# Weight loads and table clears in shorter DRAM rows, in a graph-attention and relational graph-convolution kernel

## The chip, the cores and the metric

The kernel runs on one core of a Trainium2 chip. The time is device microseconds (us) of one execution, taken as the median of several executions. All arithmetic is float32. In the profile PE is TensorE, DVE is VectorE, ACT is ScalarE, POOL is GpSimd and SP is SyncE, which in this kernel only issues DMAs. One queue of the DMA engines, q1, carries what SP issues; another, q0, carries what POOL issues. Sixteen DMA engines serve all queues. MB and GB are decimal, KB is 1024 bytes.

## The reference

Two layers run one after the other on 384 nodes with 12,672 edges, and each adds its result to its input. The first is attention in 16 heads with a mask built from the edges; the second is two relational graph convolutions with six relations that share four basis matrices.

```python
h = jnp.maximum(_layernorm(x), 0.0)                       # x: 384 x 1024
q = h @ wq.T + bq;  k = h @ wk.T + bk;  v = h @ wv.T + bv
q2, k2, v2 = heads(q @ wiq.T + biq), heads(k @ wik.T + bik), heads(v @ wiv.T + biv)
mask = full((N, N), -inf).at[src, dst].set(softplus(edge_type_weights)[edge_type - 1])
attn = softmax(q2 k2^T / 8 + mask)                        # per head
x = x + (attn v2) @ wo.T + bo

h = jnp.maximum(_layernorm(x), 0.0)
y = relu(h @ w_in + b_in)                                 # 384 x 768
for l in range(2):
    W = einsum('rb,bio->rio', comp[l], basis[l])          # 6 relations, 4 bases
    msg = einsum('ni,rio->rno', y, W)[edge_type, src] / counts[edge_type, dst]
    y = batchnorm(relu(segment_sum(msg, dst) + y @ root[l] + bias) + y)
x = x + layernorm(y @ w_out + b_out)
```

## The kernel before

**Sparse edges become dense tables in DRAM.** `mtab0` to `mtab3` hold the attention mask (384 x 384 cells each); `atab0` and `atab1` hold, for each relation, how many edges go from one node to another (6 x 384 x 384 cells each). SP first clears them from SBUF tiles (`clear_mask`, L182, and `clear`, L274: 576 KB for each DMA). Then POOL scatters 128 edges at a time: 99 DMAs of `put_mask` (L264) and 99 of `put_count` (L269). The second kind adds to the cell, four bytes for each edge. A `put_count` on one of the two tables waits until the earlier one on the same table has landed.

**POOL's queue is in program order.** It issues the mask scatters and 14 count scatters while the projections run, then loads the mask (L311), then issues the other 85 count scatters, and only then loads the adjacency counts into SBUF as the tile `A` (six relations, 576 KB each): `atab1` is copied into `A[:, r]` (L834 for r = 0, 1, L838 for the others) and `atab0` is added to it by an accumulating DMA (L836). Between these, `add_up(r)` (L339, L340) sums the three node blocks of `A[:, r]` on POOL into the tile `sum`.

**TensorE needs these sums.** In the first graph convolution (layer 0 in what follows), `share(r)` (L345) is a pair of matmuls that adds `sums[r]` over the partitions; the result gives the reciprocal edge count, with which DVE scales `A[:, r]`. The dictionary `between` places `share(0)`, `share(1)`, `share(2)` inside the products of basis 2 of layer 0, `share(3)` after them, `share(4)` and `share(5)` inside the products of basis 3. PE runs in program order too, so a share that isn't ready holds up all that follows. After basis 3, `mix` (L330, L332) combines the six relations into the four matrices `At`.

**Weights come through one queue and one pool.** `wload` (L76 to L81; its DMA is L80) takes one of five buffers of `wpool` and issues a load on SP. A projection of the attention layer uses four loads of 1 MB, a basis matrix or `root` three loads of 768 KB (a third of 768 x 768), `w_out` three of 1 MB. `w_in` is loaded by two DMAs of 1.5 MB at L734. SP waits at a load until its buffer is free, and the loads run ahead of the products that use them. The products are recursive (Strassen-like) ones: DVE first forms differences of the weights (L380, L555, L771, L911, L913, L919), then PE multiplies. The basis products are L969 and L963.

**Layout.** On the host each weight is arranged so that one load gives each of the 128 partitions one contiguous row: 8 KB for the attention projections and `w_out`, 12 KB for `w_in`, 6 KB for `basis` and `root`. A clear writes 4.6 KB (1,152 floats) for each partition.

Of the kernel before, what the change touches and what calls it, by code (L numbers as in the profile page):

```python
# [10 lines left out]
F32 = mybir.dt.float32  # L11
# [18 lines left out]
HN = N // 2  # L30
R = 6
# [11 lines left out]
MCELLS, ACELLS = N * N, N * R * N  # L43
# [8 lines left out]
def gnn_kernel(ctx: ExitStack, tc: tile.TileContext, out, x, edges, chunks, cols, rows, small,  # L52
               wq, wk, wv, wiq, wik, wiv, wo, w_in, basis, root, w_out):
    nc = tc.nc
# [5 lines left out]
    wpool = ctx.enter_context(tc.tile_pool(name="wpool", bufs=5))  # L60
# [9 lines left out]
    def next_bank(name, among=range(8)):  # L70

        i = next(i for i in ring if i in among)
        ring.remove(i)
        ring.append(i)
        return bank(i, name)

    def wload(src, name):

        w = wpool.tile([P, *src.shape[1:]], F32, tag="w", name=name)
        nc.sync.dma_start(w, src)  # L80
        return w  # L81

    turn = [0]
# [88 lines left out]
    mtab = [tables.tile([MCELLS + P, 1], F32, name=f"mtab{i}") for i in range(MT)]  # L172
    atab = [tables.tile([ACELLS + P, 1], F32, name=f"atab{i}") for i in range(2)]
    keys_d = tables.tile([PAD, P], I32, name="keys_d")

    def edge_steps(ep, none, zero):
# [2 lines left out]
        nc.sync.dma_start(small_sb, small.to_broadcast([P, 52]))  # L179

        def clear_mask(i):
            nc.sync.dma_start(mtab[i][:MCELLS, :].rearrange("(p f) o -> p (f o)", p=P), none)  # L182

        clear_mask(0)
        clear_mask(1)
# [11 lines left out]
        part = ep.tile([P, 1], F32, name="part")  # L197
# [73 lines left out]
                                         count[:, 1, c:c + 1], None, compute_op=ALU.add)  # L271

        def clear(i, r):
            nc.sync.dma_start(atab[i][:ACELLS, :].rearrange("(r p f) o -> r p (f o)", p=P, r=R)[r], zero)  # L274

        counts = enumerate(j * PER + r for r in range(PER) for j in range(tables_in(r)))

# [78 lines left out]
    with ExitStack() as inner:  # L356
        ap = inner.enter_context(tc.tile_pool(name="attn", bufs=2))

        def act_tile(name):
            return ap.tile([P, KD, N], F32, tag="T", name=name, bufs=4)  # L360
# [32 lines left out]
        def project(w, src, bias, name, on_part=None, on_start=None):  # L393

            dst = act_tile(name)
            for part in range(4):
                wt_ = wload(w[part], f"w_{name}")
                ps = [next_bank(f"ps_{name}") for _ in range(2)]

                cuts = (slice(0, HN), slice(HN, N)) if src is hT and part == 0 else (slice(0, N),)  # L400
                for c in cuts:
                    for o in range(2):
                        for k in range(KD):
                            nc.tensor.matmul(ps[o][:, c], wt_[:, k, o * P:(o + 1) * P], src[:, k, c],  # L404
                                             start=(k == 0 and c.start == 0), stop=(k == KD - 1 and c.stop == N),
                                             skip_group_check=True)
                        if on_start:
                            on_start = on_start()
                for o in range(2):
                    oc = part * 2 + o  # L410
                    nc.scalar.activation(dst[:, oc, :], ps[o][:, :N], AF.Identity,
                                         bias=cols_sb[:, bias + oc:bias + oc + 1])
                fill(1)
                if on_part:
                    on_part(part, dst)
            return dst

        def fill(n):

            for _ in range(n):  # L420
                if next(steps, "end") == "end":
                    break

        boB = ap.tile([P, D], F32, name="boB", bufs=1)
        with tc.tile_pool(name="edge", bufs=1, side="right") as ep:
            none = ep.tile([P, NT * N], F32, tag="V1", name="none")
            nc.gpsimd.memset(none, 8.0 * NEG)
            zero = ep.tile([P, NT * N], F32, tag="V2", name="zero")
            nc.gpsimd.memset(zero, 0.0)
            xn = ap.tile([P, NT, D], F32, tag="T", name="xn", bufs=4)  # L430
            with tc.manual_schedule(engines={mybir.EngineType.Activation}):
# [6 lines left out]
                half = lambda t: lambda j: x_sb[:, t, j * 512:(j + 1) * 512]  # L438
# [27 lines left out]
            def prepare():  # L466

                name, w, _, part = plan[len(loaded)]
                wt_ = wload(w[part], f"w_{name}")
                loaded.append([[wt_[:, i * 4:i * 4 + 4, o * P:(o + 1) * P] for i in range(2)] for o in range(2)])  # L470
                S.append(output_sums(loaded[-1], ep.tile([P, 4, 4, P], F32, tag="S", name="S", bufs=2)))

# [10 lines left out]
            for n, (name, w, bias, part) in enumerate(plan):  # L483
                src = {"q2": q, "k2": made.get("k")}.get(name, hT)
                if part == 0:
                    dst = made[name] = act_tile(name)
# [5 lines left out]
                a, s = loaded[n], S[n]  # L492
# [34 lines left out]

            wv2 = [[wload(wiv[half, j], "w_v2") for j in range(2)] for half in range(2)]  # L530

            def va(i, j):

# [87 lines left out]

        prA = keep.tile([P, KD, N], F32, tag="hT", name="prA")
        prB = soft.tile([P, KD, N], F32, name="prB")
        w_o = [[wload(wo[half, j], "w_o") for j in range(2)] for half in range(2)]
        attT = act_tile("attT")
        scale = 1.0 / math.sqrt(HD)
        STEPS = (H // 2) * NT
# [87 lines left out]
        for g in range(STEPS + 1):  # L715
            f = g + LEAD
            if g < STEPS:
                turn_probs(g)
            if f < STEPS:
                exponents(f)  # L720
            if f - 1 in total:
                normalise(f - 1)
            if f + 1 < STEPS:
                scores(f + 1)
            if g == STEPS:
                ps_y = next_bank("ps_y", (0,))
                multiply_o(ps_y, 2, 0, range(KD - 1))
            if g > 0:
                gather(g - 1)
            if f + 2 == STEPS:  # L730

                w_x = [act_tile("w_x") for _ in range(2)]
                for half in range(2):
                    nc.sync.dma_start(w_x[half], w_in[half])  # L734
                w_first = [wload(basis[0, 0, part], "w_c") for part in range(3)]
                w_first += [wload(basis[0, 1, part], "w_c") for part in range(2)]
        soft_stack.close()
        xtp = ctx.enter_context(tc.tile_pool(name="xtp", bufs=2, side="right"))

# [6 lines left out]
        a = [[[w_x[oc // 3][:, i * 4:i * 4 + 4, oc % 3 * P:(oc % 3 + 1) * P] for i in range(2)]  # L746
              for oc in (2 * p, 2 * p + 1)] for p in range(3)]
# [108 lines left out]
        for p in range(3):  # L856
            s = S[p % 2]
# [32 lines left out]
    with tc.tile_pool(name="conv", bufs=1) as cp:  # L890
# [31 lines left out]
        w_first = [w_first[:3], w_first[3:]]  # L922

        def load_basis(l, b):
            w = w_first.pop(0) if w_first else []
            return w + [wload(basis[l, b, part], "w_c") for part in range(len(w), 3)]


        def shares(*rs):
# [17 lines left out]
        w = load_basis(0, 0)  # L947
        T = weight_sums(w)
        for l in range(L):
# [3 lines left out]
            for b in range(B):  # L953
# [38 lines left out]
                if b + 1 < B:  # L992
                    w = load_basis(l, b + 1)
# [1 line left out]
                go_between(l, b, 4)  # L995


            w = [wload(root[l, part], "w_c") for part in range(3)]
            XN = xtp.tile([P, KC, N], F32, tag="XT", name="XN")
            pr = [next_bank("ps_c", [i for i in range(8) if i not in kept])[:, :N] for _ in range(KC)]  # L1000
            for k in range(KC):
# [8 lines left out]
            if l + 1 < L:  # L1010
# [4 lines left out]
                w = load_basis(l + 1, 0)  # L1015
# [136 lines left out]

        for t in range(NT):
            nc.gpsimd.tensor_tensor(x_sb[:, t, :], x_sb[:, t, :], rowsB[:, 2, :], ALU.add)  # L1154
        w = [wload(w_out[part], "w_out") for part in range(3)]
        hf_ = cp.tile([P, NT, D], F32, tag="H", name="hf")
        for t in range(NT):
            hf = hf_[:, t, :]
# [26 lines left out]
def _by_outputs(w, n):  # L1185

    *lead, i, o = w.shape
    w = w.reshape(*lead, i // P, P, n, o // n)
    m = len(lead)
    return w.transpose(*range(m), m + 2, m + 1, m, m + 3)  # L1190


def _by_rows(w, n):

    *lead, i, o = w.shape
    w = w.reshape(*lead, n, i // P // n, P, o)
    m = len(lead)
    return w.transpose(*range(m), m, m + 2, m + 1, m + 3)


def _by_inputs(w):

    i, o = w.shape
    return w.reshape(2, i // P // 2, P, 2, o // 2).transpose(3, 0, 2, 1, 4)


def _column(v):

    return v.reshape(-1, P).T
# [35 lines left out]
```

## Time and profile before

| | |
|---|---|
| median of 3 runs | 732.62 us (730.12 to 734.74) |
| the profiled execution, its own time | 729.42 us |
| its span in the trace | 727.6 us |
| DVE busy | 515.2 us (71%) |
| POOL busy | 311.9 us (43%) |
| ACT busy | 157.6 us (22%) |
| granted TensorE clock, mean | 0.99 |
| bytes moved by DMA | 91.00 MB, mean 125 GB/s |
| queue q1 (issued by SP) | 17,678 packets, 78.44 MB, 30.5% of 16 engines |
| queue q0 (issued by POOL) | 21,296 packets, 9.60 MB, 11.2% of 16 engines |

PE is the busy engine, so a change in the time has to come from a moment at which PE isn't working, or is working slower. The table says only how much of the span each engine used; where PE stands still, and for whom, is read from the views of waits, of the chain that ended last and of the time line. A packet in the DMA views is one piece of a transfer on one DMA engine. For SP's loads the counts show that it is one contiguous row: three basis loads of 128 rows of 6 KB each appear as 384 packets of that size, and 48 small ones, 16 for each load.

### The profile page before, as it was taken

Reading aid. Unit: us, or ns where it says so; the run is one execution under the profiler, and the core shown is the slowest. Engines: PE = TensorE matmul, PEld = TensorE weight load, DVE = VectorE, ACT = ScalarE, POOL = GpSimd, SP = SyncE. Lnnn points to the kernel's source line nnn. Section 1 sums busy time; section 2 is a strip of 40 time slices with the busy share of each in tenths; the row PEclk is TensorE's granted clock in tenths of the full one; section 3 lists DMA queues with packets and bytes.
Section 4 is the critical chain, followed back from the end, with each engine's and each line's share of the span. In section 5 each row is a group of like instructions: output and inputs, shape, how many; then the busy total and the mean of one; then the engine's idle time right before and its main releaser. Section 6 shows DMA issues by size and latency. Waiting matters only on the chain.

```text
span 727.6 us, 8832 instructions
## 1 busy us (share of the span) xinstructions
PE 703.3 (97%) x3228; PEld 528.8 (73%) x3228; DVE 515.2 (71%) x1307; ACT 157.6 (22%) x360; POOL 311.9 (43%) x239
## 2 busy tenths in 40 slices
PE   8999999999999999999999959999999999999995
PEld 7759999999996444488975535558975555579943
DVE  5886697969876799777444338899878676506756
ACT  3211111111112587300211115201131111011100
POOL 1366677778676688586785654100000000030000
PEclk9999999999999999999999989999999999999998
DMA  8786786274535522634324699221103213700001
GB/s 298 263 337 203 232 253 212 55 239 135 172 81 154 144 3 1 217 44 96 37 1 130 178 221 250 91 83 44 43 1 130 79 57 125 292 11 1 1 29 58
DMA packets 40024, 91.00 MB, mean 125 GB/s; under 512 B 19644, under 2 KB 26912, under 8 KB 35758
## 3 DMA queue, kind: packets, MB, share of 16 engines
q1 hardware_dynamic: 17678, 78.44, 30.5%
q0 software_dynamic: 21296, 9.60, 11.2%
q10 hardware_dynamic: 1008, 2.41, 0.9%
q8 instruction: 25, 0.41, 0.2%
q14 instruction: 17, 0.14, 0.1%
HBM read 79.27 MB, written 11.16 MB: 124 GB/s over the span
## 4 chain that ended last, share of the span: by engine, by line
PE 84%; DVE 9%; DMA 3%; ACT 2%; POOL 1%; issue 1%; SPq 0%; DVEq 0%; ACTq 0%
PE ps_g L969 11%; PE ps_k L386 10%; PE ps_c L1061 9%; PE ps_g L963 9%; PE ps_v L386 8%; PE ps_q L404 6%; PE ps_q L386 5%; PE ps_f L1167 4%; DVE At L332 4%; PE ps_y L386 3%; PE ps_c L1003 3%; PE ps_x L386 3%; DMA A<-atab 2%; PE ps_o L691 2%; PE ps_s L646 2%; PE ps_pT L680 2%
## 5 line engine op out<-in xcount | busy, mean ns | idle before, releaser
L269 POOL DMA_INDIRECT atab<-count,at x99 | 166.2, 1679 | 59.1 <-DMA atab<-count,at 32.2
L264 POOL DMA_INDIRECT mtab<-m_val,at x99 | 104.9, 1060 | 62.3 <-issue 25.2
L1154 POOL TENSOR_TENSOR x_sb<-x_sb,room 128x1024 f32<-128x1024 f32 x3 | 7.0, 2352 | 177.6 <-DMA room<-in_rows 177.6
L332 DVE SCALAR_TENSOR_TENSOR At<-A,small_sb,At 128x1152 f32<-128x1152 f32 x40 | 53.6, 1411 | 0.0
L969 PE MATMUL ps_g<-w_c,XT 128*128 128x384 f32 x144 | 49.2, 496 | 0.0
L963 PE MATMUL ps_g<-T,S 128*128 128x384 f32 x144 | 49.1, 486 | 0.0
L969 PE MATMUL ps_g<-w_c,XN 128*128 128x384 f32 x144 | 47.7, 487 | 1.1 <-DVE XN L1091 1.1
L404 PE MATMUL ps_q<-hT,w_q 128*128 128x384 f32 (+1 forms) x160 | 43.4, 436 | 1.4 <-DVE hT L97 1.4
L969 PEld LDWEIGHTS ps_g<-w_c,XT 128*128 128x128 f32 x144 | 28.1, 195 | 19.8 <-issue 1.8
L969 PEld LDWEIGHTS ps_g<-w_c,XN 128*128 128x128 f32 x144 | 27.3, 190 | 20.2 <-DVE XN L1091 1.4
L963 PEld LDWEIGHTS ps_g<-T,S 128*128 128x128 f32 x144 | 27.3, 190 | 19.2 <-ACT H L975 0.4
L404 PEld LDWEIGHTS ps_q<-hT,w_q 128*128 128x128 f32 x160 | 30.2, 200 | 14.1 <-ACT hT L90 1.7
L1061 PE MATMUL ps_c<-At,H 128*128 128x192 f32 x216 | 36.4, 326 | 0.0
L1061 PEld LDWEIGHTS ps_c<-At,H 128*128 128x128 f32 x216 | 35.4, 190 | 0.5
L386 PE MATMUL ps_k<-T,S 128*128 128x192 f32 x192 | 35.1, 326 | 0.0
L1091 DVE TENSOR_TENSOR XN<-XN,ps_c 128x192 f32<-128x192 f32 x38 | 12.5, 349 | 30.8 <-ACT XN L1047 19.7
L386 PEld LDWEIGHTS ps_k<-T,S 128*128 128x128 f32 x192 | 31.9, 190 | 0.0
L1167 PE MATMUL ps_f<-w_out,XN 128*128 128x512 f32 (+1 forms) x84 | 31.1, 531 | 0.0
L253 DVE SCALAR_TENSOR_TENSOR same<-keys,key,weigh 128x128 f32<-128x128 int32 x99 | 28.0, 348 | 0.9 <-DVE same L253 0.9
L659 DVE CUSTOM_DVE_ANT_0 s<-ps_s,mask 128x384 f32<-128x384 f32 x48 | 24.5, 549 | 5.2 <-PE ps_s L646 5.2
L253 DVE SCALAR_TENSOR_TENSOR same<-cells,own,later 128x128 f32<-128x128 int32 x99 | 27.9, 350 | 0.4
L1167 PEld LDWEIGHTS ps_f<-w_out,XN 128*128 128x128 f32 x84 | 15.9, 190 | 14.9 <-issue 14.3
(298 smaller groups left out, 1418.3 us busy)
## 6 DMA issues: line engine op xcount, KB each, us to landing
w_c<-in_basis SPq DMA_DIRECT2D x24, 768.0 KB
atab<-zero SPq DMA_DIRECT2D x12, 576.0 KB
A<-atab POOLq DMA_DIRECT2D x12, 576.0 KB
w_c<-in_root SPq DMA_DIRECT2D x6, 768.0 KB
w_q<-in_wq SPq DMA_DIRECT2D x4, 1024.0 KB
w_q<-in_wiq SPq DMA_DIRECT2D x4, 1024.0 KB
w_k<-in_wk SPq DMA_DIRECT2D x4, 1024.0 KB
w_k<-in_wik SPq DMA_DIRECT2D x4, 1024.0 KB
```

Of the source, the lines that this page charges most:

```text
L253: nc.vector.scalar_tensor_tensor(same, row[:, n, :], mine[:, c:c + 1], times, ALU.is_equal, ALU.mult, accum_out=count[:, i, c:c + 1])
L264: nc.gpsimd.indirect_dma_start(mtab[c // PER][:, :], bass.IndirectOffsetOnAxis(at[:, 0, c:c + 1], 0), m_val[:, c:c + 1], None)
L269: nc.gpsimd.indirect_dma_start(atab[0 if i < 11 else i % 2][:, :], bass.IndirectOffsetOnAxis(at[:, 1, c:c + 1], 0), count[:, 1, c:c + 1], ...
L332: nc.vector.scalar_tensor_tensor(At[:, b], A[:, r], w, At[:, b], ALU.mult, ALU.add)
L386: nc.tensor.matmul(ps, a[:, k, :], b[:, k, :], start=start and k == 0, stop=(k == 3), skip_group_check=not start)
L404: nc.tensor.matmul(ps[o][:, c], wt_[:, k, o * P:(o + 1) * P], src[:, k, c], start=(k == 0 and c.start == 0), stop=(k == KD - 1 and c.stop ...
L659: nc.vector.tensor_tensor_reduce(s[j], ps[:, :N], mask8[:, t, :], -scale, 3.0e38, ALU.add, ALU.min, tops[:, j:j + 1])
L963: nc.tensor.matmul(ps, x[:, c], y(c), start=start and c == 0, stop=(c == 2), skip_group_check=not start)
L969: nc.tensor.matmul(ps, block(XT, n, i)[:, c], w[c][:, i, o * HC:(o + 1) * HC], start=(first and c == 0), stop=(c == 2 and (i == 1 or ps is ...
L1003: nc.tensor.matmul(pr[o], w[k // 2][:, k % 2, o * P:(o + 1) * P], XT[:, k, :], start=(k == 0), stop=(k == KC - 1))
L1061: nc.tensor.matmul(ps, x[:, c], y[:, c], start=start and c == 0, stop=stop and c == 5, skip_group_check=True)
L1167: nc.tensor.matmul(p, XT[:, k, t * P:(t + 1) * P], w[k // 2][:, k % 2, c0:c1], start=(k == 0), stop=(k == KC - 1))
```

## The change

`wload` now gets the shape of the tile beside the source, and `load_rows` reads a source of shape (n, 128, size) as n short rows for each partition, in the order of the partition's row. On the host `_short` stores such a source: `wk`, `wv`, `wiq`, `wik`, `wiv` and `wo` in rows of 512 floats (2 KB), `w_in` and `basis` in rows of 384 floats (1.5 KB). `wq`, `root` and `w_out` keep their layout and are loaded as before. The clears of the tables write three rows of 384 floats for each partition in place of one of 1,152. Bytes, destinations in SBUF, the number of DMAs and the order of all instructions on every engine stay the same.

```diff
-    def wload(src, name):
-
-        w = wpool.tile([P, *src.shape[1:]], F32, tag="w", name=name)
-        nc.sync.dma_start(w, src)
+    def load_rows(dst, src):
+
+        if len(src.shape) == 3 and src.shape[1] == P:
+            n, _, size = src.shape
+            nc.sync.dma_start(dst.rearrange("p k o -> p (k o)").rearrange("p (n s) -> p n s", n=n),
+                              src.rearrange("n p s -> p n s"))
+        else:
+            nc.sync.dma_start(dst, src)
+
+    def wload(src, shape, name):
+        w = wpool.tile([P, *shape], F32, tag="w", name=name)
+        load_rows(w, src)
         return w
...
         def clear_mask(i):
-            nc.sync.dma_start(mtab[i][:MCELLS, :].rearrange("(p f) o -> p (f o)", p=P), none)
+            nc.sync.dma_start(mtab[i][:MCELLS, :].rearrange("(c p f) o -> p c (f o)", p=P, c=NT),
+                              none.rearrange("p (c f) -> p c f", c=NT))
...
         def clear(i, r):
-            nc.sync.dma_start(atab[i][:ACELLS, :].rearrange("(r p f) o -> r p (f o)", p=P, r=R)[r], zero)
+            nc.sync.dma_start(atab[i][:ACELLS, :].rearrange("(r c p f) o -> r p c (f o)", p=P, c=NT, r=R)[r],
+                              zero.rearrange("p (c f) -> p c f", c=NT))
...
                 for half in range(2):
-                    nc.sync.dma_start(w_x[half], w_in[half])
-                w_first = [wload(basis[0, 0, part], "w_c") for part in range(3)]
-                w_first += [wload(basis[0, 1, part], "w_c") for part in range(2)]
+                    load_rows(w_x[half], w_in[half])
+                w_first = [wload(basis[0, 0, part], (2, DC), "w_c") for part in range(3)]
+                w_first += [wload(basis[0, 1, part], (2, DC), "w_c") for part in range(2)]
...
+def _short(w, size):
+
+    *lead, _, a, b = w.shape
+    w = w.reshape(*lead, P, a * b // size, size)
+    m = len(lead)
+    return w.transpose(*range(m), m + 1, m, m + 2)
...
-        **{k: _by_outputs(g0(k).T, 4) for k in ("wq", "wk", "wv", "wiq", "wik")},
-        **{k: _by_inputs(g0(k).T) for k in ("wiv", "wo")},
-        "w_in": _by_outputs(g1("w_in"), 2),
-        **{k: _by_rows(g1(k), 3) for k in ("basis", "root", "w_out")},
+        "wq": _by_outputs(g0("wq").T, 4),
+        **{k: _short(_by_outputs(g0(k).T, 4), 512) for k in ("wk", "wv", "wiq", "wik")},
+        **{k: _short(_by_inputs(g0(k).T), 512) for k in ("wiv", "wo")},
+        "w_in": _short(_by_outputs(g1("w_in"), 2), HC),
+        "basis": _short(_by_rows(g1("basis"), 3), HC),
+        **{k: _by_rows(g1(k), 3) for k in ("root", "w_out")},
```

The other calls of `wload` get the shape of their tile in the same way.

More of the change, by code (lines that the diff above doesn't have):

```diff
@@ L396, in project @@
             for part in range(4):
-                wt_ = wload(w[part], f"w_{name}")
+                wt_ = wload(w[part], (KD, 2 * P), f"w_{name}")
                 ps = [next_bank(f"ps_{name}") for _ in range(2)]
@@ L468, in prepare @@
                 name, w, _, part = plan[len(loaded)]
-                wt_ = wload(w[part], f"w_{name}")
+                wt_ = wload(w[part], (KD, 2 * P), f"w_{name}")
                 loaded.append([[wt_[:, i * 4:i * 4 + 4, o * P:(o + 1) * P] for i in range(2)] for o in range(2)])
@@ L526, in gnn_kernel @@
             q2, k2, v = made["q2"], made["k2"], made["v"]
-            wv2 = [[wload(wiv[half, j], "w_v2") for j in range(2)] for half in range(2)]
+            wv2 = [[wload(wiv[half, j], (4, 512), "w_v2") for j in range(2)] for half in range(2)]
             def va(i, j):
@@ L623, in gnn_kernel @@
         prB = soft.tile([P, KD, N], F32, name="prB")
-        w_o = [[wload(wo[half, j], "w_o") for j in range(2)] for half in range(2)]
+        w_o = [[wload(wo[half, j], (4, 512), "w_o") for j in range(2)] for half in range(2)]
         attT = act_tile("attT")
@@ L925, in load_basis @@
             w = w_first.pop(0) if w_first else []
-            return w + [wload(basis[l, b, part], "w_c") for part in range(len(w), 3)]
+            return w + [wload(basis[l, b, part], (2, DC), "w_c") for part in range(len(w), 3)]
         def shares(*rs):
@@ L995, in gnn_kernel @@
                 go_between(l, b, 4)
-            w = [wload(root[l, part], "w_c") for part in range(3)]
+            w = [wload(root[l, part], (2, DC), "w_c") for part in range(3)]
             XN = xtp.tile([P, KC, N], F32, tag="XT", name="XN")
@@ L1154, in gnn_kernel @@
             nc.gpsimd.tensor_tensor(x_sb[:, t, :], x_sb[:, t, :], rowsB[:, 2, :], ALU.add)
-        w = [wload(w_out[part], "w_out") for part in range(3)]
+        w = [wload(w_out[part], (2, D), "w_out") for part in range(3)]
         hf_ = cp.tile([P, NT, D], F32, tag="H", name="hf")
```

## The prediction

> **What bounds the kernel now.** I read four views, from the whole to one moment. First the busy times and what PE waits for (engine, line, releaser: us in total, times, longest).
>
> ```profile
> PE 703.3 (97%) x3228; PEld 528.8 (73%) x3228; DVE 515.2 (71%) x1307; ACT 157.6 (22%) x360; POOL 311.9 (43%) x239
> ```
>
> ```profile
> PE ps_cnt L345 <- POOL sum L340: 7.3, 2, 6.3
> PE ps_q L404 <- DVE hT L97: 1.4, 1, 1.4
> ...
> PE ps_v L386 <- ACT v L502: 1.3, 1, 1.3
> ```
>
> PE stands still for only 24.3 us, some 11 of them before its first products and after its last, and in no row does it wait for a weight. The one large wait is for POOL's sums of A: `share(0)` and `share(1)`. Next PE's time line there (start, us, what, idle before):
>
> ```profile
> 416.96 2.10 PE L963 MATMUL ps_g<-T,XT 128*128 128x384 f32 x6
> 425.32 1.65 PE L345 MATMUL ps_cnt<-sum,ones 128*128 128x384 f32 x2 [6.26 <-POOL sum L340]
> 426.76 5.34 PE L969 MATMUL ps_g<-w_c,XT 128*128 128x384 f32 x12
> 433.17 0.91 PE L345 MATMUL ps_cnt<-sum,ones 128*128 128x384 f32 x2 [1.07 <-POOL sum L340]
> 433.92 4.03 PE L969 MATMUL ps_g<-w_c,XT 128*128 128x384 f32 x12
> ```
>
> Without the stall, the group that starts at 433.92 would start after six products (1.94 from start to start), two shares (0.65 each, as at 437.79) and twelve products (3.87): 416.96 + 1.94 + 0.65 + 3.87 + 0.65 = 424.07. The stall costs 433.92 - 424.07 = **9.85 us**. Besides the waits this holds the slow clock that follows them: twelve products take 5.34 in place of 4.03, and the windows view grants 0.75 and 0.56 at 420 to 430.
>
> The chain that ended last shows what made the sums late (start, us, what):
>
> ```profile
> 407.47 0.81 POOL A L834
> 408.28 5.52 DMA A<-atab
> 413.80 1.43 issue
> 415.23 0.78 POOL A L836
> 416.01 11.62 DMA A<-atab
> ```
>
> POOL reaches the loads of A only at 407.47, since its 99 count scatters come first, and then the loads land slowly. POOL's own time line shows why it is so late:
>
> ```profile
> 389.07 1.55 POOL L269 DMA_INDIRECT atab<-count,at  x1 [0.30 <-issue]
> 391.30 1.56 POOL L269 DMA_INDIRECT atab<-count,at  x1 [0.68 <-DMA atab<-count,at]
> 398.07 1.72 POOL L269 DMA_INDIRECT atab<-count,at  x1 [5.22 <-DMA atab<-count,at]
> ```
>
> An undisturbed scatter follows the last after 0.30 us. Here one waits 5.22 for an earlier one, while SP's three basis loads of 388.77 to 390.06 land.
>
> **What the Trainium skill says.** "DMA: Bandwidth & Descriptors", section "Queues, rings and completion order": each DMA engine goes round robin over the queues that have work, a whole packet at a time. The trace agrees and shows what a packet is. In 295 to 296, beside `w_in` (12 KB rows), and in 299 to 300, beside the start of a basis load (6 KB), the DMA view has
>
> ```profile
> q1 hardware_dynamic: 40, 0.39, 96.5%
> q0 software_dynamic: 40, 0.00, 6.8%
> ...
> q1 hardware_dynamic: 48, 0.38, 95.0%
> q0 software_dynamic: 48, 0.00, 8.1%
> ```
>
> So each 4-byte packet of a scatter waits for one whole row of a weight. SP loads whose rows are short already exist: the key broadcasts of L241, in 1.5 KB runs, give in 112 to 113
>
> ```profile
> q1 hardware_dynamic: 232, 0.37, 100.1%
> q0 software_dynamic: 98, 0.00, 12.4%
> ```
>
> that is, five times as many turns in a us at nearly the same bytes.
>
> Same page, "Why small descriptors are slow (HBM only)": about 3 cycles for each packet beside one for each 32 bytes, and 32 bytes of metadata. From that I estimate 51/48 against 195/192 cycles, 4.6% more for 1.5 KB rows than for 6 KB, and 1.6% more for metadata. The trace is rougher: basis loads run at some 400 GB/s, the key broadcasts between 228 and 377, though these read the same few DRAM rows for every partition.
>
> "TensorE: Matmul & The Clock Gate", section on the HAM clock gate: an idle window of about 3.4 us halves the clock until a busy one has passed. The 6.26 us gap and the 0.56 after it agree.
>
> **The change part by part.**
>
> *Scatters beside weight loads.* From 230 to 407 POOL waits longer than 0.30 for a scatter twelve times beside a load of the changed weights: 0.81, 1.44, 1.36, 1.74 (`wo`), 5.71, 1.57 (`w_in` and basis), 0.64, 0.95, 1.37, 2.25, 0.68, 5.22 (basis). The sum is 23.74, less 12 x 0.30 = 20.1 us. Rows get 4 times shorter (`w_in` 8 times). If each wait shrinks with them, a quarter stays, 5 us, and POOL arrives 15 us earlier. The other bound: of the wait around 391 some 2.4 us pass from the end of the issue (390.6) to the scatter's first packet (393.0); if that entry doesn't shrink, some seven bursts keep 1.4 each over the usual 1, and 10 us are won. I take 12: the loads of A start near 395.
>
> *Loads of A.* In 413.7 to 418 the accumulating load issued at 412.41 gets 27 packets, the basis loads issued from 410.06 get 276; it lands at 423.2, after 10.8. The one issued at 433.06, with no basis load in flight, is used at 439.9, after 6.8. With POOL 12 us ahead the first accumulation is issued near 400, ahead of the 410 loads; the last (442.55, landed 455.0 beside `root`, whose 6 KB rows stay) comes near 430, ahead of `root`'s loads. I count nothing more for either; both are margin.
>
> *Deadlines.* Sums 0 to 5 were ready at 425.3, 433.1, 437.2, 442.0, 448.7, 458.1. A PE without stalls asks for them at 418.9, 423.4, 427.9, 436.3, 443.0, 447.6. They must come earlier by 6.4, 9.7, 9.3, 5.7, 5.7 and 10.5. Twelve us meet all, so the stall goes whole: **-9.85 us**. Next late is DVE's mix (L332, 26.6 us in the chain from 471) beside `root`'s products; it starts when basis 3 ends, moves with PE, and keeps PE's small waits of 0.34 and 0.78.
>
> *Weights landing later.* Three basis loads issued at 555.89 move 2.36 MB by 563; the first is needed by DVE (L911) at 562.52, the same in the other stages: 6.6 us for 786 KB. At 400 GB/s that is 2.0 us of transfer, at the slowest key rate (228) 3.4, with about 1.5 before and after it: no stall. The projections' loads have 9 us or more (`wv` part 3: issued 174.24, used 185.08). Beside A's loads, which take half the turns, the 410.06 load gets perhaps 150 GB/s, 5.2 us, and may come 1 us after DVE's 416.69; PE needs its rows at 424.1. Zero.
>
> *Issue on SP.* A load of 512 pieces takes 0.38 us to issue (keys at 36.69), one of 128 takes 0.33; SP has idle time everywhere. *Clears*: 4.6 KB rows become 1.5 KB on SP's queue, beside mask scatters that end by 211, while DVE first reads the mask at 225. *Start*: `wq` stays. All zero.
>
> Sum: the profiled execution took 729.42, span and 1.8 around it; less 9.85 that is 719.6. The median of the runs shown stands 3.2 higher, 732.62, which would give 722.8. Part of those 3.2 may be a longer stall of the same kind, which would go too. I forecast **722 us**.
>
> **Rivals.**
> 1. *Half the way.* The waits shrink less, or earlier loads of A fall on the burst of 389 to 396 and delay it in turn; A moves 4 to 8 us. For: sum 5 needs 10.5, the largest shift of all. Against: two margins left uncounted. 725 to 730.
> 2. *Nothing moves.* A queue's turn might in truth be bounded by what the engine has fetched ahead, in bytes, so that short rows gain no turns. For: the 2.4 us of entry and the 27 packets, which plain alternation doesn't explain. Against: 232 and 98 beside the keys. About 732.
> 3. *Slower.* The short rows of one partition are taken as one packet after all, so a scatter's piece waits behind a whole load's share, while short rows also move slower: at 300 in place of 400 GB/s every burst lasts a third longer. Scatter waits follow the bursts, 20.1 x 1/3 = 6.7 later, and all of it reaches PE, because the sums already decide there. 739. It loses against the before from the point at which short rows cost more rate than they win turns. Against: the counts beside the keys again.
> That the rows don't get shorter in the transfer is excluded as far as the keys' 1.5 KB packets show the same form of load.
>
> **How the numbers follow.** Forecast 0.72, half 0.11, nothing 0.09, slower 0.08. About 1%, 7.3 us, is what a measurement can tell from no change. The forecast's own spread, 718 to 726, lies mostly beyond that: 0.68 of faster, with a few of rival 1's cases; the rest of both and the nothing case are the same, 0.24; slower 0.08. The range reaches from 717.5 (the stall gone in the lower runs, some 2 us of other small waits too) to 731 (all of the half cases, some of the nothing ones).
>
> **What would show it.** PE's wait at L345 for POOL disappears and the clock stays at 1.00 in 415 to 435; the first L834 is issued near 395; waits of L269 for its own DMA fall from 32.2 us to some 10; q1 has over 100 packets in a us beside basis loads, q0 the same where scatters run. If L834 stays near 407, the turns were not won; if it comes early and PE still waits at L345, the loads of A are at fault; if PE or DVE waits for a weight, the rate is.

## The result, and the profile after

| | before | changed kernel |
|---|---|---|
| median of 20 runs each | 730.0 us (724.98 to 736.25) | 726.79 us (720.17 to 730.59) |
| ratio, 95% interval | | 0.9963 [0.9941, 0.9986] |
| measured again later (e11), 23 and 12 runs | 728.47 us | 725.44 us, 0.9949 [0.9924, 0.9974] |
| span of the profiled execution | 727.6 us | 725.1 us |

A ratio need not be the quotient of the medians beside it: the medians are of all executions, and the ratio leaves out those more than 1.5% above the fastest of their kernel, three of e3's eleven and of e4's eight, four of e6's twenty and of e7's twelve, one of e5's fourteen.

The change wins some 3 us where 10 were forecast. The lines of the changed kernel stand some ten further down: L269 is now L278, L345 is L355, L834 is L844. First the busy times on the page and then what PE waits for (engine, line, releaser: us in total, times, longest):

```profile
PE 701.5 (97%) x3228; PEld 527.8 (73%) x3228; DVE 515.1 (71%) x1307; ACT 157.6 (22%) x360; POOL 308.3 (43%) x239
```

```profile
PE ps_cnt L355 <- POOL sum L350: 8.0, 2, 6.7
PE ps_q L414 <- ACT hT L98: 1.4, 1, 1.4
```

The one large wait of before is still there, two times, and no shorter (7.3 before). PE's time line at the place of the stall (start, us, what, idle before):

```profile
413.82 2.10 PE L973 MATMUL ps_g<-T,XT 128*128 128x384 f32 x6
422.62 1.65 PE L355 MATMUL ps_cnt<-sum,ones 128*128 128x384 f32 x2 [6.71 <-POOL sum L350]
424.07 5.45 PE L979 MATMUL ps_g<-w_c,XT 128*128 128x384 f32 x12
430.81 0.91 PE L355 MATMUL ps_cnt<-sum,ones 128*128 128x384 f32 x2 [1.29 <-POOL sum L350]
431.56 4.03 PE L979 MATMUL ps_g<-w_c,XT 128*128 128x384 f32 x12
```

By the sum used for before, the stall is now 431.56 - (413.82 + 1.94 + 0.65 + 3.87 + 0.65) = 10.63 us, after 9.85. PE arrived 3.1 us earlier (413.82 after 416.96) and then stood for longer, so that it goes on only 2.4 us earlier (431.56 after 433.92). That is all the profile won. POOL's time line says why:

```profile
385.81 1.56 POOL L278 DMA_INDIRECT atab<-count,at  x1 [0.30 <-issue]
387.67 1.55 POOL L278 DMA_INDIRECT atab<-count,at  x1 [0.30 <-issue]
393.49 1.74 POOL L278 DMA_INDIRECT atab<-count,at  x1 [4.26 <-DMA atab<-count,at]
...
404.82 1.63 POOL L844 DMA_DIRECT2D A<-atab  x2 [0.26 <-ACT H L990]
409.86 1.32 POOL L846 DMA_DIRECT2D A<-atab  x1 [3.41 <-DMA A<-atab]
```

The loads of A start at 404.82 in place of 407.47 (forecast: 395), and where a scatter waited 5.22 beside three basis loads, one still waits 4.26. Each of these waits is for the scatter before the last one, which adds to the same table: before, for the one issued from 389.07 to 390.62, now for the one issued from 385.81 to 387.36. The DMA view shows when that scatter's packets begin. Before, in 393.5 to 393.75 and in 393.75 to 394 (packets, MB, share of 16 engines):

```profile
q1 hardware_dynamic: 16, 0.10, 93.7%
...
q1 hardware_dynamic: 20, 0.12, 118.7%
q0 software_dynamic: 4, 0.00, 2.7%
```

In the changed kernel two stages of the wait, first in 390 to 391 and then in 392 to 393:

```profile
q1 hardware_dynamic: 266, 0.40, 106.0%
q0 software_dynamic: 1, 0.00, 0.2%
...
q1 hardware_dynamic: 240, 0.35, 102.5%
q0 software_dynamic: 98, 0.00, 15.0%
```

So SP's rows are short, over 200 of them land in a us, and once the scatter's pieces move, they do get more frequent turns (98 in place of 40 to 48). But the first packet comes no sooner. Before, no packet of q0 starts from 391 to 393.75, so the first comes 3.1 to 3.4 us after the end of the issue. Now none starts from 387 to 390.75, and a single one by 391: 3.4 to 3.6 us. With nothing beside it, a scatter of the kernel before whose issue ended at 386.89 had its first packets in 387.25 to 387.5, after 0.4 to 0.6 us.

Of the waits of POOL by releaser, the one of L278 for its own transfers stayed at 31.9 us after 32.2; it was to fall to some 10.

**What a single profile can't tell.** POOL's 198 scatters begin at 27.81 in the profile of before and at 26.28 after, so 1.5 of the 2.65 us lie ahead of every changed weight load. From the first scatter to the last it takes 377.9 us before, 376.7 and 374.8 in two profiles of the changed kernel. The waits of the count scatters for their own transfers differ as much: 29.5 us in the second profile of the changed kernel, and 25.9 in that of e5 below, whose weights have long rows. That the change wins 3 us is read from the medians, not from these, and no profile of the kernel shows that the 3 us come off these waits.

### The profile page after: what moved, and what is told of

Same layout as the page of the kernel before. It is cut to its first block, busy times and chain, and to the rows that moved or that the text cites. A ratio compares the mean times of both kernels' runs of the same rounds, so it can differ in the third digit from the quotient of the medians.

```text
span 725.1 us, 8832 instructions
## 1 busy us (share of the span) xinstructions
PE 701.5 (97%) x3228; PEld 527.8 (73%) x3228; DVE 515.1 (71%) x1307; ACT 157.6 (22%) x360; POOL 308.3 (43%) x239
## 4 chain that ended last, share of the span: by engine, by line
PE 84%; DVE 9%; DMA 3%; ACT 2%; POOL 1%; issue 1%; DVEq 0%; ACTq 0%; POOLq 0%
PE ps_g L979 11%; PE ps_k L396 10%; PE ps_c L1071 9%; PE ps_g L973 9%; PE ps_v L396 8%; PE ps_q L414 6%; PE ps_q L396 5%; PE ps_f L1177 4%; DVE At L342 4%; PE ps_y L396 3%; PE ps_c L1013 3%; PE ps_x L396 3%; DMA A<-atab 2%; PE ps_o L701 2%; PE ps_s L656 2%; PE ps_pT L690 2%
## 5 line engine op out<-in xcount | busy, mean ns | idle before, releaser
L278 POOL DMA_INDIRECT atab<-count,at x99 | 163.2, 1648 | 57.2 <-DMA atab<-count,at 31.9
L414 PE MATMUL ps_q<-hT,w_q 128*128 128x384 f32 (+1 forms) x160 | 41.8, 422 | 1.4 <-ACT hT L98 1.4
L414 PEld LDWEIGHTS ps_q<-hT,w_q 128*128 128x128 f32 x160 | 28.5, 190 | 14.1 <-ACT hT L98 1.7
L396 PEld LDWEIGHTS ps_k<-T,S 128*128 128x128 f32 x192 | 31.9, 190 | 0.0
## 6 DMA issues: line engine op xcount, KB each, us to landing
w_q<-in_wq SPq DMA_DIRECT2D x4, 1024.0 KB, 11.8
```

What stands on the lines that cost most here:

```text
L278: nc.gpsimd.indirect_dma_start(atab[0 if i < 11 else i % 2][:, :], bass.IndirectOffsetOnAxis(at[:, 1, c:c + 1], 0), count[:, 1, c:c + 1], ...
L396: nc.tensor.matmul(ps, a[:, k, :], b[:, k, :], start=start and k == 0, stop=(k == 3), skip_group_check=not start)
```

## The experiments

### Does the end follow POOL's arrival, and how much is there to win?

e1 is the kernel before, e9 the changed kernel, each with the last eight count scatters left out of the computation:

```diff
-        for i in range(EC - len(DEALT)):
+        for i in range(EC - len(DEALT) - 8):
             put_count()
```

> The kernel before without the last 8 of its 99 count scatters (their edges are missing from the table), so POOL reaches the loads of A 8 x 1.86 = 14.9 us earlier. If the prediction's step from POOL's lateness to PE's stall is right, the stall of 9.85 us goes whole: ratio 0.986 to 0.988, PE's wait at L345 for POOL under 1 us. Rival: the loads of A are slow by themselves when they come earlier (they meet the basis loads of 389 to 396), and a stall of 3 us or more stays: ratio 0.990 to 0.996.

> The changed kernel with the last eight count scatters left out of the computation, the same edit as e1 made to the kernel before, so that POOL reaches the loads of A well ahead of need in both. Theory (all that the change wins passes through POOL's arrival): nothing is left to win, ratio to the kernel before 0.981 to 0.985 as e1 (0.983), no wait of PE for POOL's sums at the shares. Rival (short rows win some time elsewhere too, for instance weights or the start): 0.976 to 0.980. Rival (short rows cost time elsewhere, which the gain at POOL hid): 0.986 to 0.990.

e1: 718.27 us, 0.9826 [0.978, 0.9872]. e9: 716.09 us, 0.9815 [0.9777, 0.9852]. The first loads of A start at 388.23 and at 382.42. PE's time line in e1, to be laid beside the one above:

```profile
416.75 2.10 PE L963 MATMUL ps_g<-T,XT 128*128 128x384 f32 x6
418.68 0.81 PE L345 MATMUL ps_cnt<-sum,ones 128*128 128x384 f32 x2
419.33 4.03 PE L969 MATMUL ps_g<-w_c,XT 128*128 128x384 f32 x12
423.20 0.81 PE L345 MATMUL ps_cnt<-sum,ones 128*128 128x384 f32 x2
423.84 4.03 PE L969 MATMUL ps_g<-w_c,XT 128*128 128x384 f32 x12
```

No idle time at either share, and all products at 4.03: the stall goes whole, as the prediction had it, if POOL is early enough. And once it is, the change wins nothing that can be told: the ratios of e9 and e1 can't be told apart, though POOL is 5.8 us earlier in e9. That fits a gain that passes through POOL's arrival. It doesn't prove it: with four executions each, the intervals reach some 0.4% to either side, as much as the whole change wins, and the medians differ by 2.2 us.

In the range measured, the rate of exchange is close to one to one. From the start of the first load of A to the end of the span there are 320.1 us before, 320.3 and 320.5 in two profiles of the changed kernel, and 319.1 to 321.4 in the profiles of e2, e3, e8 and e10 below, with arrivals from 401.52 to 407.47. (e5's profile has 323.8; PE was late there for other reasons too.) In e1, where POOL no longer decides, there are 329.2. By this sum an arrival near 717.4 - 320 = 397 would have been enough, which is an estimate.

### Which part of the change wins the 3 us?

e5 has only the clears in short rows, e8 only the weights:

```diff
# e8, against the changed kernel (e5 keeps these two, and takes back the rest)
-            nc.sync.dma_start(mtab[i][:MCELLS, :].rearrange("(c p f) o -> p c (f o)", p=P, c=NT),
-                              none.rearrange("p (c f) -> p c f", c=NT))
+            nc.sync.dma_start(mtab[i][:MCELLS, :].rearrange("(p f) o -> p (f o)", p=P), none)
...
-            nc.sync.dma_start(atab[i][:ACELLS, :].rearrange("(r c p f) o -> r p c (f o)", p=P, c=NT, r=R)[r],
-                              zero.rearrange("p (c f) -> p c f", c=NT))
+            nc.sync.dma_start(atab[i][:ACELLS, :].rearrange("(r p f) o -> r p (f o)", p=P, r=R)[r], zero)
```

> The kernel before with only the clears in three rows of 1.5 KB. The clears lie beside mask scatters and end before 150, so if the gain of the change comes from the weights, this is the kernel before: ratio 0.998 to 1.002, first load of A near 407. If the clears bring it: 0.994 to 0.998, and POOL's count scatters begin 2 us earlier.

> The changed kernel with the clears of both tables back in long rows, so that only the weights have short ones. Theory (the small gain belongs to the weights: their rows bring POOL to the loads of A some 2 to 3 us earlier, the clears do nothing): ratio to the kernel before 0.995 to 0.998, as the whole change, and the page's waits of POOL for its count scatters near 32 us. Rival (the gain lies in the clears, or only in both together): 0.999 to 1.001. Rival (the clears cost what the weights win): below 0.993.

e5, whose clears are short and whose weights are as before: 728.58 us, 0.9992 [0.9964, 1.0019]. e8: 725.13 us, 0.9945 [0.9914, 0.9976], beside the whole change at 0.9949. The clears bring nothing that can be measured; the weights bring, within the intervals, all of it. e5's one profile has POOL at the loads of A at 401.02, 6.5 us ahead of before, with the weights' rows unchanged: so much can one execution differ from another, and in this one PE was late too (2.7 us at `ps_k` for ACT, 2.1 for nothing that shows), with a span of 724.9.

### Why doesn't a scatter's wait shrink with the rows?

m1 and m2 move data only and leave the whole network out: scatters of 128 numbers into two tables on POOL, as `put_count` issues them, beside loads of 768 KB on SP, as `wload` issues them. In short (m1 has eight scatters, m2 ten):

```python
for i in range(loads):
    load(nc.sync, kind, i)     # rows of 6 KB, 1.5 KB or 512 B
for j in range(2, 12):
    scatter(j)                 # into table j % 2
```

> The kernel only moves data: it writes x to the output unchanged and measures scatters (128 x 4 bytes, adding) and accumulating loads (576 KB) beside three 768 KB weight loads in rows of 6 KB, 1.5 KB or 512 bytes, beside one load, and beside three loads of which each is issued when the one before has landed. Theory of turns (the prediction's): the longest wait of a scatter is some 5 us beside 6 KB rows, some 1.3 beside 1.5 KB, under 1 beside 512 bytes. Theory of what is fetched ahead: the wait is that of the bytes already queued, so 6 KB and 1.5 KB rows differ by less than a third (the drain of 128 pieces), and the wait falls by more than half only where one load is in flight at a time. For the accumulating load the same: 10 us against some 7 by turns, 9 to 10 in both cases by what is fetched ahead.

> Moves data only, none of the network: ten scatters of 128 numbers into two tables beside 1, 2, 3, 4 or 6 loads of 768 KB issued together just before them, in 6 KB or 1.5 KB rows; with six, also scatters that start some 2 us later, and loads issued half by SP and half by ACT. Read: how long after its issue a scatter moves its first packet (the entry), and the sum of the waits of the scatters of a group. Theory (a scatter enters only behind what is already queued, so the lock-out grows with the bytes ahead): longest wait near 1.5, 3, 4.5 to 5.5, 6 to 7 and 9 to 11 us for 1, 2, 3, 4 and 6 loads, nearly alike in both row lengths, and about 2 us less where the scatters start later. Rival (the entry is a fixed delay of some 3 to 4 us under load, after which packets alternate one to one): from three loads on the entry stays at 3 to 4 us, with 1.5 KB rows the longest wait stays at 4 to 5 us, with 6 KB rows two or more scatters wait, their sum growing with the loads, and a later start changes no wait. Rival (plain alternation, my prediction's step): the longest wait in 1.5 KB rows is a quarter of that in 6 KB rows.

The longest wait of a scatter (us; a scatter with nothing beside it follows after 0.30), in the three rounds of each:

| loads ahead | 6 KB rows | 1.5 KB rows | 512 B rows |
|---|---|---|---|
| m1: 3 | 5.42, 4.80, 5.02 | 4.25, 4.38, 4.17 | 4.06, 3.25, 3.28 |
| m1: 1 | 1.84, 1.66, 1.56 | 1.46, 1.54, 1.54 | |
| m2: 1 | 1.49, 1.57, 1.57 | 1.47, 1.63, 1.66 | |
| m2: 2 | 3.74, 3.57, 3.56 | 3.51, 3.65, 3.51 | |
| m2: 3 | 5.37, 4.08, 5.38 | 4.22, 4.26, 4.30 | |
| m2: 4 | 5.52, 5.36, 5.37 | 4.47, 4.41, 4.32 | |
| m2: 6 | 5.50, 5.20, 5.20 | 4.32, 4.48, 4.69 | |

A quarter of the row length takes at most some 20% off a wait, where the prediction took 75%; a twelfth (512 bytes) takes some 30% off. With six loads the wait is that of three or four: it doesn't grow with all that SP has queued, so m2's first theory falls too. m2's scatters with six loads show what a wait consists of; first those in 6 KB rows, then those in 1.5 KB rows:

```profile
166.57 1.55 POOL L66 DMA_INDIRECT atab<-val,at_sb  x1 [0.16 <-issue]
168.43 1.54 POOL L66 DMA_INDIRECT atab<-val,at_sb  x1 [0.30 <-issue]
175.47 1.54 POOL L66 DMA_INDIRECT atab<-val,at_sb  x1 [5.50 <-DMA atab<-val,at_sb]
177.47 1.54 POOL L66 DMA_INDIRECT atab<-val,at_sb  x1 [0.46 <-DMA atab<-val,at_sb]
181.16 1.54 POOL L66 DMA_INDIRECT atab<-val,at_sb  x1 [2.16 <-DMA atab<-val,at_sb]
...
300.77 1.55 POOL L66 DMA_INDIRECT atab<-val,at_sb  x1 [0.16 <-issue]
302.62 1.55 POOL L66 DMA_INDIRECT atab<-val,at_sb  x1 [0.30 <-issue]
308.49 1.55 POOL L66 DMA_INDIRECT atab<-val,at_sb  x1 [4.32 <-DMA atab<-val,at_sb]
310.34 1.55 POOL L66 DMA_INDIRECT atab<-val,at_sb  x1 [0.30 <-issue]
314.79 1.55 POOL L66 DMA_INDIRECT atab<-val,at_sb  x1 [2.91 <-DMA atab<-val,at_sb]
```

The DMA view of the same run, in 170 to 171 and 173 to 174 (6 KB), then 304 to 305 and 307 to 308 (1.5 KB):

```profile
q1 hardware_dynamic: 71, 0.41, 101.7%
...
q1 hardware_dynamic: 71, 0.38, 97.6%
q0 software_dynamic: 69, 0.00, 10.9%
...
q1 hardware_dynamic: 267, 0.39, 105.6%
...
q1 hardware_dynamic: 213, 0.33, 98.7%
q0 software_dynamic: 138, 0.00, 21.8%
```

**Entry.** The first scatter's issue ends at 168.12 (6 KB) and 302.32 (1.5 KB). In quarters of a us the view has its first packets at 171.5 and at 306.0: 3.4 and 3.7 us later, in which q1 has the engines to itself. (With no load beside it, m2's first packets come in the quarter that begins 0.4 us after the end of the issue.) **Passage.** Once in, its packets alternate with the 6 KB rows one to one (69 to 71 in 173 to 174), and two scatters take 4.5 us, to 176; beside 1.5 KB rows, which give 138 in a us, they take some 3, to 309. Only the passage is seen to follow the rows. The next pair of scatters, issued from 308.49, starts again from nothing: its first packets come at 313.25, 3.2 us after the end of the issue. Then they too alternate one to one, as in 313.5 to 314:

```profile
q1 hardware_dynamic: 95, 0.15, 96.0%
q0 software_dynamic: 95, 0.00, 31.8%
```

So m2's first rival holds in the main point (with six loads the first wait stays, and a second pair waits again). Its last clause wasn't tested well: the scatters meant to start 2 us later started only some 0.3 us later against the loads, and their longest waits in the first round were 5.07 and 4.24. With half of the six loads issued by ACT the longest waits rose to between 6.70 and 6.97 in 6 KB rows and between 4.83 and 5.47 in 1.5 KB rows. The first packets still came 3.5 to 4.0 us after the issue; what grew is the passage, in which three queues now take turns.

m1 also has a load of 576 KB that adds into its destination, as L836 does. The next operation on POOL waits for it 4.99 us with nothing beside it, 9.53 after three loads in 6 KB rows, 9.01 in 1.5 KB, 7.95 in 512 B, and 5.28 where each of the three 6 KB loads is issued only when the one before has landed:

```profile
221.44 0.19 POOL L92 TENSOR_TENSOR summed<-A 128x1 f32<-128x1 f32 x1 [4.99 <-DMA A<-ctab]
238.67 0.19 POOL L92 TENSOR_TENSOR summed<-A 128x1 f32<-128x1 f32 x1 [9.53 <-DMA A<-ctab]
255.40 0.19 POOL L92 TENSOR_TENSOR summed<-A 128x1 f32<-128x1 f32 x1 [9.01 <-DMA A<-ctab]
...
285.95 0.19 POOL L92 TENSOR_TENSOR summed<-A 128x1 f32<-128x1 f32 x1 [5.28 <-DMA A<-ctab]
```

The slow first load of this kind in the kernel (10.8 us from the start of its issue before, 10.7 after) looks the same, and shorter rows hardly mend it either.

### Shorter still

e4 has every shortened weight in rows of 512 bytes:

```diff
-        "basis": _short(_by_rows(g1("basis"), 3), HC),
+        "basis": _short(_by_rows(g1("basis"), 3), 128),
# likewise 128 for the attention weights and w_in
```

> The changed kernel with all the shortened weights in rows of 512 bytes. Theory of what is queued ahead: a scatter still waits for the loads issued before it; POOL reaches the first load of A within 2 us of the changed kernel (404.8), and the span is that moment plus 320: ratio to the kernel before 0.992 to 1.000. Theory of turns: the drain gets shorter again, POOL comes 5 us or more earlier than in the changed kernel, ratio under 0.990.

734.94 us, 1.0053 [1.0018, 1.0088]: slower than before, which neither theory had. The one profile is of the longest of eight executions (744.50 us), so it can't say what the others lose. SP's time line in it shows where the delay begins there (start, us from the first start to the last end, what, loads):

```profile
36.75 9.36 SPq L81 DMA_DIRECT2D w_q<-in_wiq  x3
46.21 4.23 SPq L283 DMA_DIRECT2D atab<-zero  x1
```

Three loads of 2,048 pieces each keep SP for 9.36 us, where the changed kernel, with 512 pieces each, needs 2.00. One such load alone is issued in 0.70 us (0.37 with 512 pieces), and of these three, which follow each other on the heels, one takes 4.61 (0.85). The clears behind them come later, and POOL waits once, for 11.8 us, for a table to be cleared. Its waits for its own count scatters stay at 31.9. m1, which has nothing of the network, has the slow issue too: of three loads in 512-byte rows (1,536 pieces each) the third took SP 3.15 us to issue, in 1.5 KB rows 0.46.

### Loads one at a time

If what lies ahead on SP's queue matters and rows don't, loads should come singly. e2 (before) and e3 (changed kernel) add a read of 4 bytes behind each basis load of the first layer, so that SP issues the next one only when this one has landed. e10 is e3 again:

```diff
# e3; e2 calls wload without the shape
+            w = list(w)
+            for part in range(len(w), 3):
+                w.append(wload(basis[l, b, part], (2, DC), "w_c"))
+                if l == 0:
+                    nc.sync.dma_start(drop[:, b * 3 + part:b * 3 + part + 1], w[-1][0:1, 0, 0:1])
```

> The kernel before with long rows; in layer 0 SP follows each basis load inside the loop by a 4-byte DMA that reads it, so that the next load is issued only when this one has landed. Theory of what is fetched ahead: scatters and accumulating loads get in between the loads; the wait of 5.2 us near 391 falls to about 2.5, the first accumulation lands 2 to 4 us after its issue earlier than before, and PE's stall shrinks by 3 to 6 us: ratio 0.992 to 0.996. Theory of turns: the rows are as long as before, so the waits stay: ratio 0.998 to 1.002.

> The same 4-byte reads put into the changed kernel with short rows. Theory of what is fetched ahead: as in the kernel before with these reads, perhaps 1 us better through the quicker drain: ratio 0.988 to 0.994. Theory of turns: no gain over the changed kernel, 0.995 to 0.998.

> e3 a second time and longer: the changed kernel, each load of a basis weight in the first layer after the first one's landing. Theory (loads spread out let the scatters in sooner, and short rows add their 2 to 3 us): ratio 0.990 to 0.994, below the changed kernel beside it by 0.3% or more. Rival (e3 was a lucky draw, and loads one at a time bring nothing, as on the kernel before): 0.995 to 0.998, the same as the changed kernel beside it.

e2: 728.26 us, 0.9992 [0.9966, 1.0018]. e3: 725.12 us, 0.9919 [0.9882, 0.9956]. e10: 724.35 us, 0.9933 [0.9902, 0.9964], beside the changed kernel (e11) at 0.9949. Both draws of this version beat the kernel before, as the changed kernel does; against the changed kernel the intervals overlap, and e10's own condition of 0.3% isn't met. So this version isn't shown to win anything over the change, and e2 not to win anything at all, though in its profile three waits of 1.00 to 1.26 us stand where one of 5.22 stood. m1 fits with how little it brings: where three loads of 1.5 KB rows come one at a time, three scatters wait, 1.52, 1.52 and 1.51, which beyond 0.30 each is 3.65 us, after 3.95 for the one that waits for three loads at once. (In 6 KB rows it is 1.51, 1.20 and 1.78, so 3.59 after 5.12; e2 could have won from that, and its ratio shows nothing.)

> The changed kernel unaltered, beside the other three on one chip: ratio 0.994 to 0.998, as it was measured first, and a profile whose span is POOL's arrival at the loads of A plus 319 to 321 us. If span and arrival don't differ by that sum again, the end isn't set there.

e11, the changed kernel again: 725.44 us, 0.9949 [0.9924, 0.9974], arrival at 402.62 and span 723.1, 320.5 apart. Both as expected.

### Asking for the sums later

If POOL can't come earlier, the shares could come later: e6 puts each of them one to three places down in the order of the products, e7 adds loads one at a time, `root`'s too.

```diff
-        between = {(0, 2, 0): shares(0), (0, 2, 1): shares(1),
-                   (0, 2, 2): shares(2), (0, 2, 4): lambda: [share(3), mix(0, 0, At)],
-                   (0, 3, 0): shares(4), (0, 3, 1): shares(5),
+        between = {(0, 2, 2): shares(0), (0, 2, 4): lambda: [share(1), mix(0, 0, At)],
+                   (0, 3, 0): shares(2, 3), (0, 3, 1): shares(4), (0, 3, 2): shares(5),
```

> The changed kernel with the six shares one to three places later in PE's order (share 0 in the third product group of basis 2, shares 1 after it, 2 and 3, 4, 5 in those of basis 3). If the end is set by the moment at which POOL delivers the sums, PE now has products to do while it waits: the waits for sums 0 to 2 go and only that for sum 5 stays (it was ready at 455.4 and would be asked for near 449, and root's loads move earlier beside it), 3 to 8 us are gained on the changed kernel: ratio to the kernel before 0.985 to 0.993. If PE's stall was not what sets the end: 0.996.

> As the run before, and in layer 0 each basis load in the loop and each load of root waits until the one before has landed (a 4-byte DMA that reads it). Theory of what is queued ahead: the accumulating loads of A are no longer held up by root, sum 5 comes 4 us earlier than with late shares alone, and the ratio is 0.982 to 0.988. Theory of turns: the same as with late shares alone.

e6: 727.22 us, 0.9972 [0.9947, 0.9997]. e7: 732.76 us, 1.0018 [0.9983, 1.0053]. Both miss, and e6 lands near the 0.996 that it gave for the case that the stall doesn't set the end. Its profile is of the fastest of twenty executions (722.44 us; four took 740 to 748). In it PE's wait for POOL falls to 1.4 us, the stall is gone for the most part, and a new wait of 3.0 us for ACT comes in:

```profile
PE ps_g L972 <- ACT H L984: 3.0, 1, 3.0
PE ps_q L414 <- DVE hT L105: 1.4, 1, 1.4
PE ps_cnt L355 <- POOL sum L350: 1.4, 1, 1.4
```

DVE waits 3.7 us for basis weights in the same profile; in e7 8.7, and PE waits 6.4 for ACT. In e7's profile, then, the weights of these stages have no room for loads one at a time. What keeps the usual execution of e6 at the time of the changed kernel is open: its profile isn't of one.

## Why the prediction was wrong

- **Where the kernel is bound: right.** The stall at the shares is where the end is set. e1 and the sum of arrival and 320 us show it; e6 says only that moving the shares isn't enough.
- **Deadlines: right in substance.** With POOL early enough the stall goes whole (e1). What that is worth agrees with the 9.85 us that were counted: the medians of e1 differ by 10.3, and the interval of its ratio reaches from 9.3 to 16. Other gains of eight scatters less may be part of it.
- **"Scatters beside weight loads": wrong, and this is the step that failed.** It read "if each wait shrinks with them, a quarter stays" and took 12 us of 20.1. The waits have two parts. The passage goes by turns, as the prediction said, but the entry, 3.4 and 3.7 us in m2, comes before any turn and isn't shorter with shorter rows; in the kernel it was 3.1 to 3.4 us before and 3.4 to 3.6 after. From m2's groups of three loads, summed over the rounds, the waits beyond 0.30 are 13.93 us in 6 KB and 11.88 in 1.5 KB rows, 15% less (20% with a gap of 1.21 us in one of the 6 KB rounds, for which the profile shows no releaser); for single loads there is no clear difference. An estimate from these, 0 to 20% of 20.1, is 0 to 4 us, and the medians moved by some 3.
- **The cautious bound was misread, in the same step.** It took 2.4 us for the entry near 391, with the first packet at 393.0, and 1 us for the usual one. In quarters of a us no packet comes before 393.75, and the two are 3.1 to 3.4 and 0.4 to 0.6. If every burst has that entry, seven of them keep at least 7 x (3.1 - 0.6) = 17.5 of the 20.1 us, and at most 2.6 are left to win in place of 10. That is an estimate, but it comes from the trace of before by the prediction's own sum, and it lies near what was measured.
- **The counts beside the keys (232 and 98 in a us)** were read as proof that short rows win a scatter's time. They were taken from the passage. A count within one us can't show how long the scatter had stood before it.
- **Loads of A as margin:** no margin came, since POOL didn't reach them ahead of the basis loads. In m1 such a load takes 4.5 us longer behind three loads in 6 KB rows.
- **Weights landing later, issue, clears, start: right** at zero for the rows chosen: no wait of PE or DVE for a weight appeared in the two profiles of the changed kernel (in e9's, with POOL early, DVE has one of 1.9 us), e5 puts the clears at nothing that can be measured, and e9 beside e1 shows no cost elsewhere that stands out of the noise. At 512 bytes the issue would have been wrong (e4).
- **Rivals:** "Nothing moves" named the right evidence, the entry and the 27 packets, and was given 0.09. It was wrong in that short rows do gain turns; what stays is the time before the first turn. "Slower" didn't happen with these rows, and did in e4; its profile points to another mechanism than the one described, the issue on SP.

Open: what the entry consists of. It might be work that the engines have already taken on from the other queue, a number of bytes rather than a time, or the fetch of the scatter's own pieces in a loaded memory. At one rate of transfer, m2 can't part these. m1's loads in 512-byte rows move fewer bytes in a us, and there too the first packet came 3.2 to 3.6 us after the issue, behind 0.9 to 1.1 MB in place of the 1.4 and 1.3 of m2's two scatters above. That speaks for a time rather than a number of bytes or of rows, in three groups only. More tables in turn, so that more scatters enter together, weren't tried.

## What to carry to other kernels

Here a small transfer beside large ones waited twice, for its first turn and then for its turns. Read the two apart, from the end of its issue to its first packet and from there to its end, and in windows much shorter than the wait, before crediting a change of the row length with either. When the end follows one engine's arrival one to one, test the size of the prize first by leaving some of that engine's work out, and the size of the lever by itself in a kernel that only moves data.

## What the runs showed of the hardware

- Beside six loads of SP a scatter of POOL had its first packet 3.4 us (6 KB rows) and 3.7 us (1.5 KB) after the end of its issue, beside three in 512-byte rows 3.2 to 3.6; alone it takes 0.4 to 0.6. A pair issued during the burst paid again (3.2 us). From three loads on the longest wait no longer grew (5.37, 5.52 and 5.50 for three, four and six in the first round of 6 KB rows).
- One load of 768 KB cost a scatter 1.2 to 1.5 us (1.46 to 1.84 less 0.30), two 3.2 to 3.4, with little or no difference between 6 KB and 1.5 KB rows.
- Once it is in, q0 gets one packet for one of q1, beside 6 KB rows (69 to 71) and beside 1.5 KB rows (95 to 95). Windows in which a scatter's packets have only begun have fewer (4 to 20 in the quarter from 393.75), and so has 307 to 308 in m2 (138 to 213).
- In e4's profile a load in 2,048 pieces took SP 0.70 us to issue by itself and 4.61 right behind another; in the changed kernel one in 512 pieces took 0.37, and up to 0.85 in the same place.
